# A four-layer graph network, 32 graphs on one core: scales read straight into rows, loads that yield to turned rows, a first chain by chunk, and a last layer 3 with features on partitions

## The chip, the cores and the metric

The kernel runs on one core of one Trainium2 chip. The core has five engines that work side by side, each through its own queue in order: TensorE (PE in the profile; PEld is its loading of weights) multiplies matrices, VectorE (DVE) and ScalarE (ACT) work on elements, GpSimd (POOL) does a few odd operations, and SyncE (SP) issues transfers (DMAs). An instruction that waits holds up everything behind it in its queue. Data live in SBUF and in eight PSUM banks, both with 128 partitions; a product takes its first operand (the weights, 128x128 here) and streams 128, 256 or 512 columns of the second past it.

The metric is the time of one execution on the device in microseconds (us), lower is better. All numbers are float32.

## The reference

There are 32 graphs ("batches") of N = 512 nodes with D = 128 features, and an adjacency matrix A (512x512) for each. Four layers follow one another; each normalizes x by rows, takes the positive part h, and adds its result to x. Cut to what matters:

```python
for layer in (L0, L1, L2, L3):
    h = relu(layernorm(x));  x = x + layer(h, A)

L0:  A1 = A + I;  r = rowsum(A1) ** -0.5
     leaky_relu((r A1 r) (h W) + b)
L1:  i, o, n = elu(h W_in + b), elu(h W_out + b), elu(h W_node + b)
     tanh([A i, n, A^T o] W_upd + b)
L2:  four sublayers on f (skip connections widen f to 1, 1, 2, 3 blocks of 128):
     f = tanh([rows_l2(A) (f ws + bs), f wn + bn, cols_l2(A)^T (f wd + bd)] wu + bu)
     # rows_l2 / cols_l2: each row / column divided by its Euclidean norm
L3:  m = tanh(A (h W_msg + b));  gi = m W_ih + b;  gh = h W_hh + b
     r, z = sigmoid(gi_r + gh_r), sigmoid(gi_z + gh_z)
     n = tanh(gi_n + r * gh_n);   out = (1 - z) * n + z * h
```

## The kernel before

**Data.** A batch's nodes are cut into four chunks of 128. `x`, `h` and the like are kept as rows (a node on each partition, four chunks side by side, 256 KB); `hT`, `f`, `agg` have features on partitions and 512 nodes along. The adjacency is read from memory twice, as `a` and as its transpose `aT` (1 MB each, by pieces of 256 KB for batch 0 and of 512 KB for the others), and `aT` a third time as `aT2` for layer 3, since layer 2 multiplies `a` and `aT` by its scales in place. An aggregation is four products of 512 columns into one bank (`ps_agg`). Layer 2's update weights are folded into the others at the start (`setup`, lines 334 to 417, from the tables `raw0`, `raw2`, `raw3`); three of its and layer 3's linear parts go by a scheme of seven products instead of eight (`seven`, lines 558 to 628).

**The order is planned.** `program(b)` does not issue anything: it records operations with `op(engine, us, ...)`, a guessed cost, what they read and write, and for a DMA its KB. `Plan.order` (lines 157 to 228) then simulates all engines and picks, on each engine, the ready operation with the smallest key:

```python
due = o.batch * PERIOD if o.batch < B - 1 else (B - 2) * PERIOD + ENDING
o.key = (due - o.tail + o.later if o.rank is None else o.rank - 1e6, i)
```

`tail` is the longest chain of costs behind an operation in its batch, `PERIOD` is 30, and `rank` puts the first loads ahead of all. Buffers come from slots (8 PSUM banks, 32 slots `s2` of 256 KB, 6 `s4` of 512 KB, 10 `s8` of 1 MB); an operation that needs a slot waits in the plan until one is free, and younger batches leave `kept` slots of each kind to older ones. So several batches are under way at once, and any change of costs, dependencies or slots can reorder every queue. `kept_warm` (line 235) puts idle products on PE where the plan has a gap of over 0.7 us. All DMAs are issued by SP, but for two small ones by ACT at the start.

**The steps that the change and the prediction touch**, by lines of the kernel before:

- `normed` (456 to 479): four row statistics on DVE (`moments`), variance to the power -0.5 on POOL into `sc` (line 466, 4 columns), the offset `nb` on DVE (474), and four normalizations `h` on ACT (478). For layer 0 the row sums of `a` come with it: `degree` (635) on ACT, four chunks of 512 columns, and the power then has 8 columns.
- `transposed` (510) gives `hT`. For batches 0, 1 and 31 by four transposing products on PE and a copy on ACT (516, 517). For all others by `turned` (483 to 501): DVE turns 32x32 blocks into `blk` (487), four DMAs of 64 KB write it to memory in another order (496), one DMA of 256 KB reads it back (500), and ACT puts the columns in order (519). The same path brings layer 2's result back to rows as `f4r`, where DVE adds it to x (784); the end batches use products instead (781).
- `own` (646): A + I needs the diagonal blocks of `aT` plus the identity: `diag`, on POOL, by chunk for batch 0.
- Layer 1: `ps_lin` is layer 0's last product, DVE applies scale and bias to it (`z`), then comes `normed`, `hT`, the products `ps_sd` of i and o, their exponents, and `rep` (691 to 695), on which the two aggregations wait. `u1` (706) is the update's sum on DVE.
- Layer 2's scales: ACT squares and sums `a` and `aT` by chunks (716 to 718), POOL takes the power -0.5 of 8 columns into `inv` (721), SP writes it to memory (`bounce`, 4 KB, line 726), and one DMA of 512 KB reads the 4 KB back to all partitions as `spaced` (730), where the 8 scales of a node lie side by side. ACT copies them apart into `rows` (735, 1024 columns), and DVE multiplies the eight chunks of `aT` and `a` by them (739). After that come four sublayers, each ended by a tanh on ACT (768).
- Layer 3: the message products and `msg`, the aggregation over `aT2`, `mT` (tanh, 801), the gate products (809 to 834) with nodes on partitions, tanh for r and z with halved arguments, and lines 842 to 859 for `u`, `n`, `w`, `q`, `xo` and the output DMA. In the last two batches this goes chunk by chunk, with the gates' biases added from broadcast rows (834), and with POOL doing two steps of `q`.

## Time and profile before

| what | us |
|---|---|
| median of nine runs | 2320.31 (2319.4 to 2323.42) |
| the profiled execution, its own time | 2321.19 |
| its span, first to last instruction | 2319.3 |
| PE busy, 9682 products | 2298.6 |
| DVE / ACT / POOL busy | 1530.4 / 946.9 / 262.0 |
| the 32 copies `rows` on ACT, each | 2.06 |
| `spaced`, issue to landing, median | 4.2 |
| `f4r`, issue to landing, median (shortest turned row read: `turned` 2.7) | 3.4 |

How to read it. The page gives each engine's busy time and its share of the span; a group's line reads: line, engine, operation, output<-inputs, shapes, count, busy time, mean in ns, idle time before it and what ended that. A timeline line reads: start in us, duration, engine, line, operation, and in brackets the idle time before it with what ended it; lines of SPq are issues of DMAs. A windows line gives the stretch, its length, and each engine's busy time with the number of instructions, then the granted TensorE clock (1.00 is full), the share of DMA time and GB/s. The granted clock is 0.999 over the whole span.

### The profile page before, as it was taken

What the parts mean: (1) busy time and instruction counts of PE and PEld (TensorE: products, weight loads), DVE (VectorE), ACT (ScalarE), POOL (GpSimd) and SP (SyncE); (2) the same over time, 40 slices, a digit from 0 to 9 for tenths busy, and PEclk for the clock granted to TensorE, in tenths of its full rate; (3) what the DMA queues carried; (4) which work ended last, traced back from release to release, by engine and by line L of the source; (5) the groups of instructions that cost most, each with busy time, mean ns of one, the idle gap of its engine ahead of it and who ended that gap; (6) DMA issues with size and microseconds to landing.
All of it is one profiled execution on the core that took longest, in us unless ns stands there. A gap on an engine that the chain in (4) does not pass through costs nothing.

```text
span 2319.3 us, 28279 instructions
## 1 busy us (share of the span) xinstructions
PE 2298.6 (99%) x9682; PEld 1445.2 (62%) x9682; DVE 1530.4 (66%) x4132; ACT 946.9 (41%) x2018; POOL 262.0 (11%) x218
## 2 busy tenths in 40 slices
PE   8999999999999999999999999999999999999998
PEld 7556666666666566666666665666666666656665
DVE  6656666666667676666666676766766666767655
ACT  8323444344443344343344433444433444334412
POOL 3001110101101011010111100110101111101101
PEclk9999999999999999999999999999999999999999
DMA  7102322223222233222332322322223322223200
GB/s 270 37 10 65 117 83 84 86 85 109 77 88 82 82 109 87 87 77 83 104 107 76 91 82 82 109 84 86 82 83 104 109 74 91 82 82 105 78 5 27
DMA packets 133054, 200.82 MB, mean 87 GB/s; under 512 B 18992, under 2 KB 79920, under 8 KB 132912
## 3 DMA queue, kind: packets, MB, share of 16 engines
q1 hardware_dynamic: 132624, 198.90, 28.3%
q8 instruction: 76, 1.25, 0.2%
q14 instruction: 66, 0.54, 0.1%
q10 hardware_dynamic: 288, 0.13, 0.0%
HBM read 160.05 MB, written 38.93 MB: 86 GB/s over the span
## 4 chain that ended last, share of the span: by engine, by line
PE 90%; DMA 4%; DVE 3%; ACT 2%; POOL 1%; SPq 1%; issue 0%; ACTq 0%; DVEq 0%
PE ps_agg L326 60%; PE ps_seven L597 11%; PE ps_sd L326 9%; PE ps_upd L326 4%; PE ps_gate L326 2%; DMA f4r<-turn_f4r 1%; PE ps_msg L326 1%; PE ps_node L326 1%; ACT h L478 1%; DMA turn_f4r<-blk 1%; PE ps_lin L326 1%; POOL sc L466 1%; SPq L496 1%; ACT f L768 1%; DVE bn L450 0%
## 5 line engine op out<-in xcount | busy, mean ns | idle before, releaser
L326 PE MATMUL ps_agg<-aT,sd 128*128 128x512 f32 x1024 | 510.2, 593 | 0.1
L326 PE MATMUL ps_agg<-a,sd 128*128 128x512 f32 x1024 | 482.4, 592 | 0.0
L466 POOL TENSOR_TENSOR sc<-v,neg_half 128x4 f32<-128x4 f32 (+1 forms) x128 | 157.7, 1232 | 1634.9 <-DVE v L453 1360.6
L326 PEld LDWEIGHTS ps_agg<-a,sd 128*128 128x128 f32 x1024 | 184.6, 190 | 182.9 <-issue 178.4
L326 PE MATMUL ps_agg<-f,w_sb 128*128 128x512 f32 x448 | 230.3, 596 | 5.4 <-ACT f L768 5.3
L326 PEld LDWEIGHTS ps_agg<-aT,sd 128*128 128x128 f32 x1024 | 177.9, 191 | 82.2 <-issue 66.0
L326 PE MATMUL ps_sd<-w_sb,f 128*128 128x256 f32 x768 | 217.4, 380 | 0.5 <-ACT f L768 0.4
L478 ACT ACTIVATE h<-xr,nb,sc 128x128 f32<-128x128 f32 x384 | 158.2, 482 | 136.6 <-DVE nb L474 136.3
L597 PEld LDWEIGHTS ps_seven<-t_sb,s 128*128 128x128 f32 x1128 | 161.5, 191 | 78.1 <-issue 69.3
L326 PEld LDWEIGHTS ps_sd<-w_sb,f 128*128 128x128 f32 x768 | 136.5, 191 | 95.3 <-issue 76.8
L597 PE MATMUL ps_seven<-t_sb,s 128*128 128x128 f32 x1128 | 168.1, 275 | 0.0
L735 ACT COPY rows<-spaced 128x1024 f32<-128x1024 f32 x32 | 66.1, 2064 | 169.9 <-DMA spaced<-bounce 169.9
L326 PE MATMUL ps_agg<-aT,rep 128*128 128x512 f32 x256 | 130.3, 593 | 2.0 <-DVE rep L693 2.0
L326 PE MATMUL ps_agg<-a,rep 128*128 128x512 f32 x256 | 130.4, 592 | 0.0
L768 ACT ACTIVATE f<-ps_agg,cf_sb 128x512 f32<-128x512 f32 x128 | 87.2, 682 | 98.7 <-PE ps_agg L326 98.7
L326 PE MATMUL ps_agg<-aT,msg 128*128 128x512 f32 x256 | 124.9, 592 | 0.0
L487 DVE STREAM_TRANSPOSE blk<-f 128x512 f32<-128x512 f32 x29 | 20.6, 711 | 139.8 <-ACT f L768 139.8
L326 PE MATMUL ps_agg<-aT,h 128*128 128x256 f32 (+2 forms) x384 | 99.1, 381 | 0.0
L597 PEld LDWEIGHTS ps_seven<-w_sb,f 128*128 128x128 f32 x512 | 75.9, 191 | 35.4 <-issue 27.7
L553 DVE TENSOR_TENSOR sd<-ps_sd,rf_sb 128x512 f32<-128x512 f32 x128 | 87.0, 680 | 15.6 <-PE ps_sd L326 15.6
L739 DVE TENSOR_TENSOR aT<-aT,rows 128x512 f32<-128x512 f32 x128 | 88.1, 688 | 13.6 <-PE ps_agg L326 13.6
L739 DVE TENSOR_TENSOR a<-a,rows 128x512 f32<-128x512 f32 x128 | 88.2, 690 | 13.1 <-PE ps_agg L326 13.0
(144 smaller groups left out, 3815.3 us busy)
## 6 DMA issues: line engine op xcount, KB each, us to landing
aT<-in_adjt SPq DMA_DIRECT2D x124, 512.0 KB, 5.2
a<-in_adj SPq DMA_DIRECT2D x62, 512.0 KB, 5.0
turn_turned<-blk SPq DMA_DIRECT2D x348, 64.0 KB, 1.8
turned<-turn_turned SPq DMA_DIRECT2D x87, 256.0 KB, 2.7
spaced<-bounce SPq DMA_DIRECT2D x32, 512.0 KB, 4.2
x<-in_x SPq DMA_DIRECT2D x32, 256.0 KB, 2.9
out<-xo SPq DMA_DIRECT2D x30, 256.0 KB, 2.0
turn_f4r<-blk SPq DMA_DIRECT2D x116, 64.0 KB, 1.8
```

The lines of the kernel that those rows point to most:

```text
L326: op("PE", t_mm(n), lambda: nc.tensor.matmul(out_of(ps.ap()), lhs(), rhs(), start=start, stop=stop), reads, [ps], later=later)
L466: op("POOL", t_pow(n), lambda: nc.gpsimd.tensor_tensor(inv.ap()[:, :n], v8.ap()[:, :n], neg_half[:, :n], op=ALU.pow), [v8, NH], [(inv, {0})])
L478: op("ACT", t_act(D, 2), lambda c=c: nc.scalar.activation(h.ap()[:, c, :], xin.ap()[:, c, :], AF.Relu, bias=nb.ap()[:, c:c + 1], scale=inv ...
L487: op("DVE", t_tt(N), lambda: nc.vector.transpose(blk.ap().rearrange("p b (c r) -> p c b r", c=NC), m.ap().rearrange("p c (b s) -> p c b s" ...
L496: nc.sync.dma_start(bounce.tile[:, k, :].rearrange("(b s) n -> s b n", b=NC), blk.ap()[k * P // NC:(k + 1) * P // NC])
L553: op("DVE", t_tt(N), lambda ps=ps, h=h: nc.vector.tensor_add(sd.ap()[:, 2 * h:2 * h + 2, :], ps.ap().rearrange("p (j v) -> p j v", j=2), s ...
L597: op("PE", t_mm(D), lambda j=j: nc.tensor.matmul(ps.ap()[:, k * H + j * D:k * H + (j + 1) * D], lhs()[:, j * P:(j + 1) * P], rhs(), start= ...
L735: op("ACT", t_act(2 * N), lambda: nc.scalar.copy(rows.ap().rearrange("p s (c n) -> p (s c) n", c=NC), spaced.ap().rearrange("p n k -> p k ...
L739: op("DVE", t_tt(N), lambda m=m, c=c, s=s: nc.vector.tensor_mul(m.ap()[:, c, :], m.ap()[:, c, :], rows.ap()[:, s, :]), [(m, {c}), rows], [ ...
L768: op("ACT", t_act(N, 1), lambda ps=ps, i=i, f_new=f_new: nc.scalar.activation(f_new.ap(), ps.ap(), AF.Tanh, bias=cf_sb[:, i:i + 1]), [ps, ...
```

## The change

The four parts of the title, and with them the plan's constants:

- **Scales.** `inv` is written into tiles of 32 columns, of which 24 are zeroed once by POOL. DVE turns them by blocks of 32x32, so that a scale's 32 nodes lie along a partition. 16 KB go to memory instead of 4, and the read to all partitions takes four pieces of 1 KB and lands in `rows` itself. The buffer `spaced` and the copy on ACT are gone; the eight multiplications read and write through a split view. There is one `s4` slot less and one `s2` more.
- **Loads yield.** A *way* is open in the plan from the turning of a row to its read back, and from the scales' power to the read of `rows`. While one is open, a load without a rank is not picked.
- **First loads.** `FIRST` lists the first 15 in order, with the loads of batches 1 and 2 among them; `aT` of batch 0 now goes ahead of `raw0`, `x` of batch 1 ahead of its `a`.
- **First chain by chunk.** In batch 0, `normed_by_chunk` sums each chunk of `a` on DVE, takes its power on POOL by one column, and makes offset and `h` for this chunk alone. `diag` is on DVE for batches 0 and 1.
- **Last batch.** `gates_turned` keeps layer 3's features on partitions: biases are added in ACT's function, nodes go in two halves, and products with plus or minus half the identity turn `q` and `nw` back to rows in PSUM, where DVE adds x. The output goes in two DMAs of 128 KB. Its bias columns come with `c_sb` (six more) and are copied and halved into `cg_sb` in `setup`.

The diff, cut (`...` where lines are left out; the older lines that are replaced are in the listing above):

```diff
-PERIOD = 30.0
+PERIOD = 28.0
+TURN = 32
+OWN = 2
+FIRST = ["x0", "a0", "aT0", "c", "raw0", "w1", "r1", "raw2", "raw3", "x1", "a1", "aT1", "x2", "a2", "aT2"]
...
+    def way(self, first, last):
+        first.opens += 1
+        last.closes += 1
...
                     item = heapq.heappop(queue)
+                    if item[1].yields and under_way:
+                        held.append(item)
+                        continue
...
+                under_way += o.opens - o.closes
...
-    ... {"bank": 8, "s2": 32, "s4": 6, "s8": 10}, {"bank": 2, "s2": 5, "s4": 0, "s8": 1})
+    ... {"bank": 8, "s2": 33, "s4": 5, "s8": 10}, {"bank": 1, "s2": 5, "s4": 0, "s8": 1})
...
     def t_pow(n):
-        return 0.9 + 0.1 * n
+        return 0.35 + 0.157 * n
...
+        op("DVE", 0.08, lambda: nc.vector.tensor_copy(cg_sb[:, 2:4], c_sb[:, C_L3 + 2:C_L3 + 4]), [CS], [CG])
+        op("DVE", 0.08, lambda: nc.vector.tensor_add(cg_sb[:, 0:2], c_sb[:, C_L3:C_L3 + 2], c_sb[:, C_L3 + 4:C_L3 + 6]), [CS], [CG])
+        op("DVE", 0.08, lambda: nc.vector.tensor_scalar_mul(cg_sb[:, 0:3], cg_sb[:, 0:3], 0.5), [CG], [CG])
...
+        def gates_turned(x3, h3T, msg, aT2, mT):
...
+            mm(ps, lambda t: t, lambda: wt(W_L3_HH + 2 * D), lambda: h3T.ap(), N, True, True, [h3T, W3])
+            ... hn.ap(), ps.ap(), AF.Identity, bias=cg_sb[:, 2:3], scale=0.5)
+            for k in range(2):      # halves of 256 nodes: aggregation, then mT = tanh
...
+            for k in range(2):
+                gate(ps_r, 0, W_L3_HH, h3T, True, False)
+                gate(ps_z, 0, W_L3_HH + D, h3T, True, False)
+                gate(ps_r, 0, W_L3_IH, mT, False, True, part)
+                gate(ps_n, 0, W_L3_IH + 2 * D, mT, True, True, part)
+                gate(ps_z, 0, W_L3_IH + D, mT, False, True, part)
+                act(rp, ..., AF.Tanh, 0, [ps_r], scale=0.5)
+                u = (rp + 1) * hn;  u = u + ps_n                      # two DVE steps
+                act(zp, ..., AF.Tanh, 1, [ps_z], scale=0.5)
+                act(n, lambda s=s: u.ap()[:, s], AF.Tanh, 3, [(u, part)])
+                q = (zp + 1) * h3T;  nw = (zp - 1) * n                # two DVE steps
+                for src, turn, start in ((q, 0, True), (nw, 1, False)):
+                    for j in range(2):
+                        mm(ps_o[j], ..., src[block 2k+j], id_half[turn], D, start, not start, ...)
+                for j in range(2):
+                    xo[2k+j] = x3[2k+j] + ps_o[j]                     # DVE
+                op("SP", 0.4, ... dma_start(out[b][:, 2 * k:2 * k + 2, :], xo ...), kb=H / 2)
...
         def load(dst, src, kb, rank):
+            name = f"{rank}{b}"
+            rank, kb = first(name), kb * (2 if name == "a0" else 1)
...
-                   [], [(dst, set(range(NC)[s]))], kb=kb / pieces, rank=None if b else rank)
+                   [], [(dst, set(range(NC)[s]))], kb=kb / pieces, rank=rank, yields=rank is None)
...
+        def normed_by_chunk(xin, out_tag):
...
+            for c in range(NC):
+                op("DVE", t_tt(N), ... tensor_reduce(stat.ap()[:, c:c + 1], a.ap()[:, c, :], AX.X, ALU.add), ...)
+                v8[NC+c] = stat[c] + 1                                # DVE
+                op("POOL", t_pow(1), ... inv[NC+c] = v8[NC+c] ** neg_half)
+                inv[2NC+c] = inv[c] * inv[NC+c];  nb[c] = -mean[c] * inv[2NC+c]   # two DVE steps
+                h[c] = Relu(xin[c] * inv[2NC+c] + nb[c])              # ACT
...
+            plan.way(m.uses[0][0], back)
...
-        hr, inv0 = normed(xt, "h", degree)
+        hr, inv0 = normed_by_chunk(xt, "h") if b < 1 else normed(xt, "h", degree)
...
+        own_engine, own_name = (nc.vector, "DVE") if b < OWN else (nc.gpsimd, "POOL")
...
-        bounce, spaced, rows = buf("bounce", (P, 2 * NC)), buf("s4", (P, P, 2 * NC), "spaced"), buf("s4", (P, 2, N), "rows")
+        bounce, rows = buf("bounce", (P, TURN)), buf("s4", (P, NC, 2, NC, TURN), "rows")
+        op("DVE", 0.1, lambda: nc.vector.transpose(turned_inv.ap(), inv.ap()), [inv], [turned_inv])
...
-            nc.sync.dma_start(spaced.ap().rearrange("p n k -> p (n k)"),
-                              bass.AP(tensor=d.tensor, offset=d.offset, ap=[[0, P], [1, 2 * N]]))
+            nc.sync.dma_start(rows.ap().rearrange("p q s c r -> p q (s c r)"),
+                              bass.AP(tensor=d.tensor, offset=d.offset, ap=[[0, P], [TURN * TURN, NC], [1, 2 * P]]))
...
-        op("ACT", t_act(2 * N), lambda: nc.scalar.copy(
-            rows.ap().rearrange("p s (c n) -> p (s c) n", c=NC), spaced.ap().rearrange("p n k -> p k n")), [spaced], [rows])
...
+        plan.way(root, op("SP", 0.4, spread, [bounce], [rows], kb=640))
...
+        if b == B - 1:
+            gates_turned(x3, h3T, msg, aT2, mT)
+            return
```

(Lines such as `u = (rp + 1) * hn` stand for an operation written out in full in the code.)

## The prediction, made before the changed kernel had run

> **What bounds the kernel now.** I read the page first: is one engine full, and where is it not?
>
> ```profile
> span 2319.3 us, 28279 instructions
> PE 2298.6 (99%) x9682; PEld 1445.2 (62%) x9682; DVE 1530.4 (66%) x4132; ACT 946.9 (41%) x2018; POOL 262.0 (11%) x218
> ```
>
> PE is busy 99% of the span, so only three things can shorten the kernel: less PE work, PE idle time, and the tail after PE's last product. The change leaves PE's work per batch as it is, so the second and third are what can be had. The windows view (PE busy first, then PEld, DVE, ACT, POOL, clock, DMA) says where PE idles.
>
> ```profile
> 500.00:1000.00 500.00, 496.39 (x2076) 310.37 (x2075) 336.31 (x904) 205.72 (x435) 54.97 (x42) 1.00 0.30 89
> 1000.00:1500.00 500.00, 499.52 (x2090) 312.77 (x2089) 339.83 (x910) 206.48 (x435) 54.50 (x42) 1.00 0.30 91
> 1500.00:2000.00 500.00, 499.96 (x2087) 312.28 (x2086) 340.89 (x914) 207.17 (x436) 54.94 (x42) 1.00 0.30 90
> ```
>
> The steady part loses almost nothing late and 3.6 us early. All windows from 60 to 2200 us together lose 6.4 us, and eight rows of idle products at 263.9 hide 0.9 more: 7.3 us. What ends these waits, by the waits view (us, times, longest) and one of the places in the timeline:
>
> ```profile
> PE ps_agg L326 <- ACT f L768: 5.3, 7, 1.5
> PE ps_agg L326 <- DVE rep L693: 2.0, 1, 2.0
> ```
>
> ```profile
> 341.58 0.39 SPq L730 DMA_DIRECT2D spaced<-bounce  x1
> 342.89 0.34 SPq L500 DMA_DIRECT2D f4r<-turn_f4r  x1
> 347.68 0.69 DVE L784 TENSOR_TENSOR xr<-xr,f4r 128x512 f32<-128x512 f32 x1 [1.55 <-DMA f4r<-turn_f4r]
> 351.91 1.65 ACT L478 ACTIVATE h<-xr,nb,sc 128x128 f32<-128x128 f32 x4 [1.46 <-DVE nb L474]
> 353.47 0.67 ACT L768 ACTIVATE f<-ps_agg,cf_sb 128x512 f32<-128x512 f32 x1
> 354.19 1.13 PE L326 MATMUL ps_agg<-f,w_sb 128*128 128x512 f32 x2 [0.98 <-ACT f L768]
> ```
>
> 512 KB of `spaced` go out 1.3 us ahead of the turned rows `f4r`, which land 4.8 us after issue; DVE waits 1.55, four normalizations reach ACT late and stand ahead of the tanh that PE waits for.
>
> The start: 33.3 us of PE work (the products before layer 2's first, by number, at 0.857 us for 512 columns, 0.43 for 256, 0.22 for 128) end at 55.2 us: 22 us lost.
>
> ```profile
> 9.87 1.65 POOL L466 TENSOR_TENSOR sc<-v,neg_half 128x8 f32<-128x8 f32 x1 [8.53 <-DVE v L640]
> 13.26 0.46 PE L326 MATMUL ps_agg<-diag,h 128*128 128x128 f32 x2 [0.93 <-ACT h L478]
> 30.47 2.06 ACT L735 COPY rows<-spaced 128x1024 f32<-128x1024 f32 x1 [0.46 <-DMA spaced<-bounce]
> 33.93 1.69 DVE L693 TENSOR_TENSOR rep<-rep,sd 128x512 f32<-128x512 f32 x1
> 35.68 1.12 PE L326 MATMUL ps_agg<-aT,rep 128*128 128x512 f32 x2 [1.99 <-DVE rep L693]
> ```
>
> The end: PE's last products start at 2311.5, and what follows takes 7.7 us.
>
> ```profile
> 2307.00 0.58 ACT L801 ACTIVATE mT<-ps_agg 128x512 f32<-128x512 f32 x1
> 2310.78 1.04 PE L326 MATMUL ps_gate<-w_sb,mT 128*128 128x128 f32 x6
> 2315.81 0.48 DVE L857 TENSOR_TENSOR xo<-q,n 128x128 f32<-128x128 f32 x2
> ```
>
> **The change part by part. Start.** The degrees move from ACT (0.63 us and a 0.19 us read each) to a DVE reduction a chunk. No row has it: between 0.43 (tensor-scalar, 512 columns) and 0.69 (tensor-tensor); I take 0.65. The one-column root lies between nothing and the 1.01 of four columns; the slope to the eight-column 1.65 gives 0.5. Last chunk of `a`: landed at 8.7, root at 10.4. But `aT` rules: its last chunk lands at 13.2 now and, with 768 KB of `raw0` behind it instead of ahead (1.9 us at the queue's 410 GB/s), at 11.3. A new copy of `c_sb` into `cg_sb` stands in DVE's queue ahead of the last two chunks and waits for `c_sb`, which lands at 11.4 now. Then two `diag` (0.28), the small ones and h (0.49): aggregation over at 14.0 instead of 17.0, so 3.0 us. From there to the products on `rep` (18.7 us now) I take off 0.7 (x of batch 1 lands before a), 1.1 (nb took 1.22 beside POOL's diag, 0.15 elsewhere; diag is on DVE here), 0.4 (copies ahead of hT), 1.3 (the 2.06 us rows copy ahead of the exponent), 1.0 (L693 was 1.69 beside POOL, 0.68 elsewhere), and add 1.2 for batch 1's diag and batch 2's statistics, which now stand ahead of `sd` on DVE and wait for their loads: products on rep at 29.4, 6.3 us earlier. Back comes 1.1: the eight multiplications by `rows` now stand ahead of `u` on DVE, and `rows` lands near 34.5, its bounce queued behind batch 2's loads: 29.8, plus 4.7 like the first `spaced` (4.88). Start: **-5.2**, between -3 (DMA rules) and -7.5 (nothing comes back).
>
> By the Trainium skill (TensorE: Matmul & The Clock Gate, What's actually happening) an idle window of about 3.4 us halves PE's clock, which speaks against 43 idle products instead of 60. Here the 1.99 us gap was followed by full-speed products, and every slice's granted clock is 9. Were a gap to pass the limit, an estimate from that page is +1.7 us.
>
> **Scales of layer 2.** Gone in each batch: the 2.06 us ACT copy; `spaced` (512 KB) moves from ahead of `f4r` to behind it. Added: a 32-column DVE transpose (between 0.13, the smallest op, and 0.71 for 512 columns; 0.15), 16 KB out instead of 4 (1.4 us to landing now; 64 KB take 1.8), and rows in pieces of 1 KB (4.2 now). Multiplications with a split view: L784 reads and writes such a view at 0.68, as L739 does its plain one at 0.69, so nothing. The rows are issued some 10 us before their readers.
>
> The Trainium skill (DMA: Bandwidth & Descriptors, Anatomy of one DMA; Specifications) gives 2.0 us plus bytes over 436 GB/s, so an estimate of 3.2 us for rows against the row's 4.2, and a penalty under 512 bytes a piece, which the bounce's 128 bytes fall under. Either leaves the readers covered, and the sum as it is.
>
> With f4r alone in the queue (2.85 us like `turned`, not 3.4 to 4.8), and layer 2's tanh ahead of f4r's normalizations on ACT, the seven ACT waits should go, and the idle at 264. The early batches (1 to 3) keep waits of their own. I take **-6.0** of 7.3, between -7.3 and -2.
>
> **The new order's own risk.** It differs in each of some 26 like batches, so a small wait counts 26 times. The tightest turned row I find is layer 1's:
>
> ```profile
> 844.61 1.11 POOL L466 TENSOR_TENSOR sc<-v,neg_half 128x4 f32<-128x4 f32 x1 [10.24 <-DVE v L453]
> 852.56 0.34 SPq L500 DMA_DIRECT2D turned<-turn_turned  x1
> 855.45 0.62 ACT L519 COPY hT<-turned 128x512 f32<-128x512 f32 x1 [3.56 <-DMA turned<-turn_turned]
> 856.88 1.03 PE L326 MATMUL ps_sd<-w_sb,hT 128*128 128x256 f32 x4
> ```
>
> From layer 0's last product (838.9) hT took 17.2 us; PE reached it at 18.0 and did not wait. In the new order PE has 14 products of 512, 3 of 256 and 17 of 128 columns between (17.0 us) instead of 13, 4 and 23 (17.9). The chain: the stream transpose of f now stands ahead of z on DVE (+0.35), sd for s (+0.2), 0.85 of other work leaves, POOL's 1.65 us root for the scales stands ahead of sc (sc at 5.95, not 5.75), and nb no longer waits behind f4r's xr (-0.8): hT at 16.7, usable at 16.85. Slack 0.15 instead of 0.7. If rows slows the four DMAs behind it as spaced slowed f4r (0.55), PE waits 0.4; if not, 0. The rows issue is 2 us ahead, so nearer to none: 0.06 a batch, **+1.5**, between 0 and +10.
>
> **Last batch.** Its products: 10 of 256, one of 512 and 8 of 128 columns for 8 and 8, +1.7 us, of which 0.9 lies in the new tail. Before the tail: 0.9 of idle products goes, 0.9 of products comes. Tail after the last gate product: 0.2, tanh 0.45, tanh 0.42, nw 0.42, products 0.6, additions 0.5, signals 0.4, then 2.6 from the last issue to the end as now: 5.6 against 7.45 now. **-1.9**, between +0.5 and -3.5.
>
> Loads that yield to turned rows: their bytes stay; slots free them 20 us and more before use in the steady part, so nothing.
>
> Sum: -5.2 - 6.0 + 1.5 - 1.9 = -11.6. The profiled execution took 2321.2 (span 2319.3 and 1.9 around it), its nine runs' median 2320.3: 2309.6 on the one, 2308.7 on the median. I say 2308.5.
>
> **Rivals.** First, *slower*: hT's wait. It alone decides from 0.5 us a batch, where 26 waits eat the 13.1 us of the other terms; at 0.65 the time is 2324. For it: a slack of 0.15 in a 17 us chain, and 512 KB ahead of four small DMAs. Against it: those rows are sent 2 us ahead, and f4r cost only 0.55 at 1.3 us. Second, *the queue rules the start*: the DMA's share is 0.94 to 1.04 from 10 to 40 us, so a shorter chain could only wait for loads: -2 instead of -5.2, 2312. Third, *the change does not do it in the middle*: f4r stays late behind out and adjacency loads, -1 instead of -6: 2314. Fourth, *all of it, no new wait*: -7.5 - 7.3 - 3.5 gives 2302.
>
> **How the numbers follow.** No change can be told within 0.2%, 4.6 us. Forecast with its spread (2303 to 2313) 0.47; the queue or the middle (2310 to 2315.5) 0.21; all of it (2298 to 2303) 0.10; a wait at hT of 0.25 to 0.5 us that leaves 2315.7 to 2322, 0.12; more than that, 0.10. Faster 0.78, same 0.10, slower 0.12 (some of the same lies near its upper bound). For 8 in 10 the range goes from 2300 to 2319.
>
> **What would show it.** Right: PE's products on rep near 29, the first layer-2 product near 50, no waits for ACT f in the middle, 1500 to 2000 as full as before, out's last issue some 3 us after the last product. Wrong: a wait of PE ps_sd for ACT hT 26 times; DVE waiting for DMA rows ahead of u well past 36; DVE stuck on c_sb past 12. The prediction falls if the period of a middle batch (70.7 us now) grows by 0.4 or more.

## The result, and the profile after

The changed kernel takes 2328.9 us (median; 2323.53 to 2334.32), where the kernel before, run beside it, took 2321.09 (2318.64 to 2323.87). The ratio is 1.0032, 95% interval 1.0024 to 1.0039: slower by 0.3%, where 2308.5 was forecast. The profiled execution took 2327.39, with a span of 2325.6 and a granted clock of 0.999 over it. The differences between traces below are differences of spans, 2319.3 and 2325.6: +6.3.

The page's first lines, of the kernel after:

```profile
span 2325.6 us, 28292 instructions
...
PE 2303.3 (99%) x9662; PEld 1443.2 (62%) x9662; DVE 1530.5 (66%) x4179; ACT 872.2 (38%) x1970; POOL 260.5 (11%) x210
```

PE is 99% busy as before, and ACT's busy time fell by 74.7 us, most of it the copies (66.1). PE's own busy time grew by 4.7 with 20 instructions fewer (each product of the program is two instructions here), which says nothing yet: the ends of products are modelled, and part of a wait can count as busy. So I compared the starts of PE's products: the time at which PE has done a given amount of work (number of products of each kind by their undisturbed times), less that work, is what is lost up to there.

| stretch, by PE's work | lost, before | lost, after | change | forecast |
|---|---|---|---|---|
| start, first 60 us of work | 22.85 | 19.51 | -3.3 | -5.2 |
| middle, 60 to 2150 us | 22.8 | 35.7 | +12.9 | -4.5 |
| end (lost -0.5, more products +1.7, tail after the last product's start -4.4) | | | -3.2 | -1.9 |
| sum | | | +6.4 | -11.6 |

Start and end gave what was promised, 6.5 us against 7.1. The middle went the wrong way by 17.4 us. Its three windows of after, with the columns of the prediction's:

```profile
500.00:1000.00 500.00, 497.84 (x2076) 310.09 (x2075) 336.47 (x913) 190.47 (x429) 56.23 (x42) 1.00 0.30 91
1000.00:1500.00 500.00, 496.60 (x2071) 308.96 (x2070) 334.15 (x909) 189.16 (x427) 55.97 (x42) 1.00 0.29 88
1500.00:2000.00 500.00, 495.71 (x2070) 308.87 (x2069) 333.76 (x908) 188.62 (x426) 56.24 (x42) 1.00 0.29 88
```

Before, the third window was full (499.96); here it is the emptiest. What PE waits for, by the waits view of after (us, times, longest):

```profile
PE ps_sd L350 <- ACT hT L638: 8.1, 12, 2.0
PE ps_agg L350 <- DVE msg L917: 3.5, 5, 1.0
PE ps_agg L350 <- DVE rep L813: 2.9, 2, 2.5
...
PE ps_agg L350 <- ACT f L891: 0.2, 1, 0.2
```

The wait for layer 2's `f` (5.3, seven times) is down to one of 0.2. In its place stand `hT` of layer 1, `msg` of layer 3, and `rep`. The starts show more than the waits view, since products behind the late one run slow too: from 70 to 2260 us, hT costs 14.1, msg 5.4, and rep with the products behind it 4.5; against that 9.4 of waits for f and of idle products went, and some 0.8 elsewhere. That closes the balance: 24.0 - 9.4 - 0.8 = 13.8, which is the growth in that stretch.

**hT.** One of the twelve places, in the timeline of after:

```profile
1770.98 0.37 SPq L853 DMA_DIRECT2D rows<-bounce  x1
1772.87 1.82 SPq L614 DMA_DIRECT2D turn_turned<-blk  x4
1778.94 0.34 SPq L618 DMA_DIRECT2D turned<-turn_turned  x1
1781.84 0.62 ACT L638 COPY hT<-turned 128x512 f32<-128x512 f32 x1 [5.66 <-DMA turned<-turn_turned]
1782.51 1.78 PE L350 MATMUL ps_sd<-w_sb,hT 128*128 128x256 f32 x7 [2.02 <-ACT hT L638]
```

The 512 KB of `rows` go out 1.9 us ahead of the four writes of 64 KB that turn layer 1's rows. SP can issue the read back only when the writes have landed; that is 6.1 us after the first write here, and 3.3 in the kernel before (median). The order is the same in all batches 4 to 30, and the times in nearly all: rows 7.7 us after the last product of layer 0, the writes at 9.65, and PE arrives at 17.1. The DMA issues show it in the medians (KB each, median us from issue to landing), first of before, then of after:

```profile
turn_turned<-blk SPq DMA_DIRECT2D x348, 64.0 KB, 1.8
...
spaced<-bounce SPq DMA_DIRECT2D x32, 512.0 KB, 4.2
...
x<-in_x SPq DMA_DIRECT2D x32, 256.0 KB, 2.9
```

```profile
turn_turned<-blk SPq DMA_DIRECT2D x348, 64.0 KB, 2.3
...
rows<-bounce SPq DMA_DIRECT2D x32, 512.0 KB, 5.3
...
x<-in_x SPq DMA_DIRECT2D x32, 256.0 KB, 6.0
...
f4r<-turn_f4r SPq DMA_DIRECT2D x29, 256.0 KB, 2.6
```

The same 512 KB take 1.1 us longer as `rows` than as `spaced`, and x takes twice as long.

**msg.** On DVE, the statistics of x of the batch after next stand some 10 us ahead of msg. Where x is late, DVE stands still, and in all five places of a wait for msg PE's product on msg starts 10.68 us after x has landed. One of DVE's waits for x:

```profile
1360.63 0.29 DVE L542 BATCH_NORM_STATS2 bn<-x 128x6 f32<-128x128 f32 x1 [3.20 <-DMA x<-in_x]
```

**The last batch.** Here `rows` go out 1.3 us ahead of the read of f4r, just as spaced did in the kernel before (timeline, then windows of after):

```profile
2192.67 0.38 SPq L853 DMA_DIRECT2D rows<-bounce  x1
2193.95 0.34 SPq L618 DMA_DIRECT2D f4r<-turn_f4r  x1
2199.85 0.69 DVE L907 TENSOR_TENSOR xr<-xr,f4r 128x512 f32<-128x512 f32 x1 [4.07 <-DMA f4r<-turn_f4r]
2203.71 1.83 PE L350 MATMUL ps_agg<-aT,rep 128*128 128x512 f32 x2 [2.46 <-DVE rep L813]
```

```profile
2202.00:2204.00 2.00, 0.29 (x1) 0.30 (x2) 2.00 (x6) 1.65 (x4) 0.00 (x0) 0.99 0.00 0
2204.00:2206.00 2.00, 2.00 (x3) 0.68 (x2) 2.00 (x5) 0.26 (x1) 0.00 (x0) 0.50 0.03 8
```

f4r lands 5.9 us after its issue instead of the median 2.6, `rep` stands behind it, PE waits 2.46, and then the granted clock is 0.50: the wait is paid a second time by products at half speed.

**Start and end**, in the timeline of after:

```profile
11.35 0.17 DVE L387 COPY cg_sb<-c_sb 128x2 f32<-128x2 f32 x1 [0.98 <-DMA c_sb<-in_bcol]
13.91 0.38 PE L350 MATMUL ps_agg<-diag,h 128*128 128x128 f32 x2
29.96 1.13 PE L350 MATMUL ps_agg<-aT,rep 128*128 128x512 f32 x2 [0.42 <-DVE rep L813]
42.21 0.16 DVE L589 TENSOR_TENSOR sc<-sc 128x4 f32<-128x4 f32 x1 [0.33 <-POOL sc L584]
42.89 0.68 DVE L826 TENSOR_TENSOR u<-ps_upd,r_sb 128x512 f32<-128x512 f32 x1
51.91 1.13 PE L350 MATMUL ps_sd<-w_sb,f 128*128 128x256 f32 x4
...
2319.32 1.03 PE L350 MATMUL ps_gate<-mT,w_sb 128*128 128x256 f32 x4
2321.37 0.71 PE L350 MATMUL ps_gate<-id_half,q 128*128 128x128 f32 x4
```

The products on rep come 5.7 us earlier than before; the first layer-2 products only 3.3, since `u` stands on DVE behind `sc` of batch 1.

### The profile page after: what moved, and what is told of

The parts are those of the page before. It is cut to its first block, busy times and chain, and to the rows that moved or that the text cites. A ratio compares the mean times of both kernels' runs of the same rounds, so it can differ in the third digit from the quotient of the medians.

```text
span 2325.6 us, 28292 instructions
## 1 busy us (share of the span) xinstructions
PE 2303.3 (99%) x9662; PEld 1443.2 (62%) x9662; DVE 1530.5 (66%) x4179; ACT 872.2 (38%) x1970; POOL 260.5 (11%) x210
## 4 chain that ended last, share of the span: by engine, by line
PE 80%; DMA 8%; DVE 6%; POOL 2%; SPq 2%; ACT 1%; issue 1%; ACTq 0%; POOLq 0%; DVEq 0%
PE ps_agg L350 53%; PE ps_seven L716 10%; PE ps_sd L350 8%; PE ps_upd L350 3%; PE ps_gate L350 3%; DMA turn_turned<-blk 3%; DMA x<-in_x 2%; DMA turned<-turn_turned 1%; SPq L614 1%; POOL sc L584 1%; DVE bn L542 1%; PE ps_msg L350 1%; PE ps_lin L350 1%; PE ps_node L350 1%; DVE sd L672 1%
## 5 line engine op out<-in xcount | busy, mean ns | idle before, releaser
L350 PE MATMUL ps_agg<-aT,sd 128*128 128x512 f32 x1024 | 503.9, 593 | 0.4 <-DVE sd L694 0.3
L350 PE MATMUL ps_agg<-a,sd 128*128 128x512 f32 x1024 | 501.9, 593 | 0.0
L350 PEld LDWEIGHTS ps_agg<-a,sd 128*128 128x128 f32 x1024 | 175.9, 191 | 114.8 <-issue 112.9
L716 PEld LDWEIGHTS ps_seven<-t_sb,s 128*128 128x128 f32 x1128 | 167.3, 191 | 92.6 <-issue 84.4
L965 ACT ACTIVATE g<-g 128x512 f32<-128x512 f32 (+1 forms) x64 | 36.1, 608 | 399.4 <-DVE g L694 398.9
L716 PE MATMUL ps_seven<-t_sb,s 128*128 128x128 f32 x1128 | 178.6, 275 | 0.0
L742 DVE TENSOR_TENSOR ev<-ps_seven,ev 128x512 f32<-128x512 f32 x94 | 65.0, 691 | 132.0 <-PE ps_seven L716 131.7
L350 PE MATMUL ps_agg<-aT,msg 128*128 128x512 f32 (+1 forms) x264 | 131.4, 583 | 3.5 <-DVE msg L917 3.5
L841 POOL TENSOR_TENSOR inv_sb<-stat,neg_half 128x8 f32<-128x8 f32 x32 | 53.0, 1657 | 677.8 <-DVE stat L840 653.3
L837 ACT ACTIVATE sq<-aT 128x512 f32<-128x512 f32 x128 | 80.1, 626 | 49.2 <-DMA aT<-in_adjt 48.2
```

Of the source, the lines that this page charges most:

```text
L350: op("PE", t_mm(n), lambda: nc.tensor.matmul(out_of(ps.ap()), lhs(), rhs(), start=start, stop=stop), reads, [ps], later=later)
L716: op("PE", t_mm(D), lambda j=j: nc.tensor.matmul(ps.ap()[:, k * H + j * D:k * H + (j + 1) * D], lhs()[:, j * P:(j + 1) * P], rhs(), start= ...
L742: op("DVE", t_tt(N), lambda: nc.vector.tensor_add(ev.ap(), bank_b.ap()[:, None, :H].to_broadcast([P, 2, H]), ev.ap()), [bank_b, ev], [ev])
L837: op("ACT", 0.73, lambda c=c, s=s, m=m: nc.scalar.activation(sq.ap(), m.ap()[:, c, :], AF.Square, accum_out=stat.ap()[:, s * NC + c:s * NC ...
L841: root = op("POOL", t_pow(2 * NC), lambda: nc.gpsimd.tensor_tensor(inv.ap()[:, :2 * NC], stat.ap(), neg_half, op=ALU.pow), [stat, NH], [inv])
L965: op("ACT", t_act(cols), lambda s=s: nc.scalar.activation(g.ap()[:, s, :2 * D], g.ap()[:, s, :2 * D], AF.Tanh, scale=0.5), [(g, fields(par ...
```

## The experiments

Each ran beside the kernel before on its chip; there the kernel before has medians from 2318.8 to 2321.3 us, so the ratios are what is compared. "Late" is how much later products start than they could, by the starts of products as above.

### Is the place of rows in the queue the cause?

The first kernel sends `rows` of batches 4 to 30 behind the next read back, the second behind the one after that; the order on all other engines stays.

```diff
-        plan.kept_warm(plan.order(), idle_products, 1.3)
+        plan.kept_warm(behind(plan.order(), lambda o: o.tag == "rows" and 3 < o.batch < B - 1, "back"), idle_products, 1.3)
```

> Change to the changed kernel: in SP's queue alone, the read of rows of batches 4 to 30 goes behind the read back of the turned row that follows it (layer 1's hT), so ahead of the four writes of the second turned row. Every other queue is as in the changed kernel (median 2328.9 us). Theory A, rows ahead of the four writes holds up layer 1's turned row: hT's waits, 14 us of PE's time in the changed kernel's trace, are gone, the four writes land 3.1 us after their first issue instead of 3.7 to 6.0. But now the second turned row's writes stand 0.4 us behind rows, the loads behind it come 1.5 us later, x lands later, DVE waits longer for it, and msg comes late in most batches instead of 5 of 27: 20 to 35 us of new waits, in all 2335 to 2350 us. Theory B, the changed order's own chain on DVE, POOL and ACT makes hT late: hT's waits stay at some 14 us, and the time is 2328 to 2350 us with PE still waiting for hT.

> As the run before, but rows goes behind the second turned row's read back too, directly ahead of the loads. Theory A: no writes of turned rows stand behind rows any more, hT's waits (14 us) are gone; the loads are issued some 0.6 us earlier than in the changed kernel but have 512 KB, 1.3 us, ahead of them, and PE comes 0.5 us earlier to msg, so x is late by about 0.5 us in many batches: msg's waits go from 5 us to some 5 to 14. In all 2316 to 2329 us. Theory B: hT's waits stay, 2329 us or more.

Measured: 2354.84, ratio 1.0158 (1.0144 to 1.0171), and 2367.72, 1.0208 (1.0194 to 1.0222). The waits view of the first, then of the second:

```profile
PE ps_agg L364 <- DVE msg L934: 21.3, 24, 1.0
...
PE ps_sd L364 <- ACT hT L653: 0.9, 2, 0.6
```

```profile
PE ps_agg L366 <- DVE msg L936: 24.5, 25, 1.0
PE ps_upd L366 <- ACT agg_in L835: 11.6, 16, 1.8
...
PE ps_sd L366 <- ACT hT L655: 1.4, 2, 0.7
```

hT is late by 1.4 and 1.9 us in all instead of 14.1: rows ahead of the writes is what made it late. But the wait moves to whatever comes behind rows: the loads of the second kernel land 8.0 (`a`) and 8.6 us (`x`) after issue instead of 5.1 and 6.0, and the msg waits, five in after, become 24 and 25. The sizes were missed, in the second kernel by some 40 us. Whoever stands behind `rows` loses 2 to 3 us (in the first kernel the writes right behind it, 5.4 us to landing instead of 3.1), far more than I had charged; so the question became what makes them so slow.

### Is it the form of the read?

The first kernel reads one piece of 4 KB for each partition instead of four of 1 KB. It takes the first 4 KB of the bounce, which are not the scales of all nodes, so its results are not the reference's; the work and its order are the same.

```diff
...
-    ap=[[0, P], [TURN * TURN, NC], [1, 2 * P]]
+    ap=[[0, P], [1, 2 * N]]
```

> One size: rows is read as one piece of 4 KB for each partition (128 pieces) instead of four of 1 KB (512 pieces), 512 KB as before, at the same place in the queue. It reads the first 4 KB of the bounce, so layer 2's scales are wrong; the work and its order are the same. If the number of pieces makes rows slow and so the writes behind it late: rows lands 4.2 us after its issue (like spaced in the kernel before) instead of 5.3, the writes behind it 0.5 to 1 us earlier, and hT's waits fall from 14 us to under 5: 2318 to 2322 us. If only the bytes count: rows 5 us or more, the same 2326 to 2332 us.

Measured: 2307.04, 0.9947 (0.9933 to 0.996), better than had been expected. `rows` take 3.7 us, the four writes 3.1 from first issue to landing, hT is late by 2.6 in all, msg by 2.8. The windows view of one us of such a read (the last two columns are the DMA engines' busy share and GB/s), of after and then of this kernel:

```profile
1057.00:1058.00 1.00, 1.00 (x9) 0.82 (x8) 0.55 (x3) 0.63 (x1) 0.48 (x1) 1.00 0.59 172
```

```profile
1050.00:1051.00 1.00, 1.00 (x4) 0.44 (x3) 1.00 (x6) 0.34 (x1) 0.00 (x0) 1.00 0.72 279
```

The next kernel has the right scales with that read: four small writes put them close together, and the last batch's rows go behind f4r.

```diff
-    nc.sync.dma_start(bounce.tile, turned_inv.ap())
+    for q in range(NC):
+        nc.sync.dma_start(bounce.tile[q], turned_inv.ap()[q * TURN:q * TURN + 2 * NC])
```

> A version that computes everything and reads rows in one piece of 4 KB for each partition: the scales are written by four DMAs of 1 KB (8 partitions each) so that they lie together, and the last batch's rows goes behind f4r. All other queues are as in the changed kernel. The three more issues on SP put rows some 1.1 us later, so 0.8 us ahead of the first turned row's writes instead of 1.9. If the pieces are the cause: rows lands under 4.2 us after issue, the writes behind it in some 3.3 us, hT's waits under 3 us, 2306 to 2311 us. If it is the distance of a 512 KB read from the writes that counts, they are held up more than before, 4 us and over, and hT waits in every batch: 2320 to 2335 us.

Measured: 2311.0, 0.9959 (0.9946 to 0.9971). The gain holds with the right scales. hT is late by 1.7 in all; msg still by 5.8, so the speed of rows is not all that makes msg late.

Is it the number of pieces, or their size? Two pieces of 2 KB (again not the scales of all nodes), and then four DMAs of 128 KB with one piece each:

```diff
...
-    ap=[[0, P], [TURN * TURN, NC], [1, 2 * P]]
+    ap=[[0, P], [2 * TURN * TURN, 2], [1, 4 * P]]
```

```diff
+    for q in range(NC):
+        nc.sync.dma_start(rows.ap()[:, q]...,
+                          bass.AP(..., offset=d.offset + q * TURN * TURN, ap=[[0, P], [1, 2 * P]]))
```

> As the run with one piece of 4 KB at the same place in the changed kernel's queue, but with two pieces of 2 KB for each partition (256 pieces, 512 KB); the scales of layer 2 are wrong again. Pieces of 1 KB: landed 5.2 us after issue, the writes behind in 3.9, hT's waits 5 to 12 us, 2319 to 2329 us. Pieces of 4 KB: 3.7, 3.1, 2 us, 2307 us. If the time goes with the number of pieces, 4.2 us to landing and hT's waits of 2 to 4 us: 2308 to 2313 us. If a limit lies between 1 and 2 KB: as with 4 KB, 3.7 us, 2305 to 2309 us.

> The changed kernel with rows read by four DMAs of 128 KB, one piece of 1 KB for each partition in each, instead of one DMA with four pieces. It computes everything. The pieces and their places in memory stay; SP issues three DMAs more, so the writes behind them start up to 0.5 us later. Theory P: each DMA has one piece for each partition and is spread over all engines: the last part lands 4.5 us or less after the first issue, the writes behind in 3.3 us, hT's waits 2 to 4 us, 2308 to 2313 us. Theory S, or 1 KB pieces as such: packets of rows still some 8 at a time, 5 us or more, 2320 to 2330 us.

Measured: 2324.81, 1.0015 (1.0006 to 1.0024), and 2327.45, 1.0037 (1.0024 to 1.005). Half the pieces at double size still take 5.1 us, and four DMAs leave hT late by 11.9 and msg by 8.9. Neither number nor size nor the one DMA explains it. What is left is where the pieces lie. The next reads the same four pieces of 1 KB, but 1040 bytes apart instead of 4096; the one after that 2560 apart. Both thus read other numbers than the scales:

```diff
-    ap=[[0, P], [TURN * TURN, NC], [1, 2 * P]]
+    ap=[[0, P], [2 * P + 4, NC], [1, 2 * P]]      # the other kernel: [5 * P, NC]
```

> The changed kernel with one number changed: the four 1 KB pieces of rows are read 1040 bytes apart in memory instead of 4096 (the scales of layer 2 are wrong; work, order and number of pieces are the same). In the changed kernel some 8 packets of rows are in flight at a time and 512 KB take 3 us, with one piece of 4 KB 13 packets and 1.3 us. Theory S, pieces 4096 (or, with 2 KB, 8192) bytes apart meet in the same part of the memory: now 3.7 to 4.2 us to landing, 2306 to 2312 us. Theory P, several pieces for each partition in one DMA are spread badly over the engines: 5 us or more to landing, 2319 to 2329 us.

> The changed kernel with the four 1 KB pieces read 2560 bytes apart (scales wrong), so over 8.5 KB, at 0, 2560, 1024 and 3584 within stretches of 4096 bytes. Place within 4096 counts: 4.2 us to landing, 2306 to 2312 us. The length of the stretch counts: between the 4.1 us of 4 KB and the 5.2 of 13 KB, 2311 to 2329 us.

Measured: 2310.05, 0.9966 (0.9955 to 0.9978), and 2316.57, 0.9988 (0.9979 to 0.9996). The first differs from after in one number of one access, in no queue's order and no instruction's shape. The DMA issues of the first, then of the second:

```profile
rows<-bounce SPq DMA_DIRECT2D x32, 512.0 KB, 4.1
```

```profile
rows<-bounce SPq DMA_DIRECT2D x32, 512.0 KB, 4.8
```

That can be had with the right scales by leaving room between the blocks in memory. 64 bytes of room (pieces 4160 apart); the same with a later place for x's statistics (below) and the last batch's rows behind f4r; and 1024 bytes (5120 apart):

```diff
-    bounce.tile = dram.tile([P, TURN], ...)
+    bounce.tile = dram.tile([NC, TURN * TURN + APART], ...)      # APART = 16, or 256 numbers
...
-    ap=[[0, P], [TURN * TURN, NC], [1, 2 * P]]
+    ap=[[0, P], [TURN * TURN + APART, NC], [1, 2 * P]]
```

> The changed kernel, complete, with one constant added: in memory 64 bytes are left free behind each group of 32 rows of the bounce, so that the four 1 KB pieces of rows lie 4160 bytes apart instead of 4096. Nothing else moves. If pieces a multiple of 4096 apart meet in the same part of the memory: rows lands some 4.1 us after issue, the writes behind it in 3.1 us, hT's waits 1 to 3 us, 2306 to 2312 us. If it is only that at 1040 bytes the pieces lie within one stretch of 4 KB and so were already open: 5 us to landing, 2320 to 2330 us.

> The same with x's statistics behind mT on DVE and the last batch's rows behind f4r. With padding 3 issues fewer on SP than in the version with one piece of 4 KB that took 2306.7: rows again 1.9 us ahead of the writes. If the padding does it: 2303 to 2307 us. If not: 2315 to 2322 us, as with x's statistics alone.

> As the padded kernel, complete, but with 1024 bytes left free instead of 64, so that the four pieces of rows lie 5120 bytes apart. With 4160 they were as slow as with 4096, and 4160 leaves them in nearly the same place within a stretch of 4096 bytes. If it counts where a piece lies within 4096 bytes (0, 1024, 2048, 3072 here, as with one piece of 4 KB or with pieces 1040 apart): rows lands in 4.2 us, 2308 to 2313 us. If it counts over how long a stretch the pieces are spread (16 KB, as in the changed kernel): 5 us, 2324 to 2340 us.

Measured: 2337.72, 1.0079 (1.0065 to 1.0093); 2327.7, 1.0035 (1.0022 to 1.0048); and 2311.51, 0.9961 (0.9947 to 0.9975). The first two are slower than both expectations. So 64 bytes do next to nothing for the speed (5.0 us). In the first, the bounce also takes longer to issue (0.52 us instead of 0.34), rows come only 1.27 us ahead of the writes, and hT is late by 21.7; 1024 bytes cure it (4.0 us, hT late by 1.9 in all).

| pieces for a partition | bytes apart | issue to landing | hT late | ratio |
|---|---|---|---|---|
| 4 of 1 KB (after) | 4096 | 5.3 | 14.1 | 1.0032 |
| 2 of 2 KB | 8192 | 5.1 | 10.4 | 1.0015 |
| 4 of 1 KB, padded | 4160 | 5.0 | 21.7 | 1.0079 |
| 4 of 1 KB | 2560 | 4.8 | 5.8 | 0.9988 |
| 4 of 1 KB | 1040 | 4.1 | 1.5 | 0.9966 |
| 4 of 1 KB, padded | 5120 | 4.0 | 1.9 | 0.9961 |
| 1 of 4 KB | | 3.7 | 2.6 | 0.9947 |

Of the two rules on trial in the last expectations, the length of memory that the pieces span fails: 5120 apart they span 16 KB and are quick. The place of each piece within 4096 bytes fits all rows but one: pieces 2560 apart were expected quick and took 4.8. There the first and the last piece share 512 of the 4096 bytes (the last one starts at 3584), which may be why; no run here shows it.

By the Trainium skill (DMA: Bandwidth & Descriptors, Latency and other measured facts) copies whose rows lie 2 to 8 MiB apart run at 164 down to 103 GB/s; with 4 MiB, 4 KiB of padding restore the full rate of 214 where 192 bytes don't; why is called an inference there. The runs agree in kind, at distances down to 4096 bytes, with 64 bytes of padding useless and 1024 enough. Which part of the memory is in the way is not shown here either.

### Do the loads that yield matter, and whence the msg waits?

Without the hold, all else as in after:

```diff
-                    if item[1].yields and under_way:
-                        held.append(item)
-                        continue
```

> The changed kernel with the rule that loads yield taken out of the plan, so that the order changes again: layer 3's aT goes ahead of f4r's writes, x between f4r's writes and its read, a behind the third turned row. The 1 KB pieces of rows still stand ahead of layer 1's turned row. Theory A (rows is the cause, yielding is not): hT's waits stay at 7 to 14 us, the waits for msg (x late) go, and PE waits for the tanh of layer 2 again because f4r has 1 MB ahead of it, 5 to 10 us: 2325 to 2338 us. Rival, the loads that yield are what made the turned rows and x late: hT's waits and msg's go, under 2318 us.

Measured: 2353.95, 1.0149 (1.0133 to 1.0165), the waits view:

```profile
PE ps_sd L347 <- ACT hT L635: 25.0, 27, 2.2
PE ps_agg L347 <- DVE sd L691: 8.5, 16, 0.6
```

That is slower than either expectation, and the waits for f did not come back. The yield is not the harm as a whole: without it layer 2's turned rows queue behind 1 MB of adjacency (5.1 us for their writes), all that follows comes later, `rows` go out 1.5 us ahead of layer 1's writes and these some 10 to 12 us after layer 0's last product instead of 9.65, and hT is late in every like batch. But x lands in 4.2 us instead of 6.0, and the msg waits are gone. The yield lets loads pile up and go in one burst, in which x takes 5.5 to 6.8 us (medians) in all kernels that have it and whose page gives a landing, but for the one with rows ahead of the loads (8.6). So I left the burst alone and moved who waits for x: for batches 5 to 30 its statistics go behind the tanh `mT` in the plan's order, and thus behind msg on DVE. First in after, then in the kernel with pieces of 4 KB:

```diff
+            if 4 < b < B - 1:
+                for o in plan.ops[first_op:first_op + 2 * NC + 1]: o.tag = "xstat"
...
-        plan.kept_warm(plan.order(), idle_products, 1.3)
+        plan.kept_warm(behind(plan.order(), lambda o: o.tag == "xstat", "mT"), idle_products, 1.3)
```

> The changed kernel, rows in pieces of 1 KB as there, with only x's statistics moved behind mT on DVE. Theory (rows makes the turned rows late, these make the loads late since SP issues in order, and DVE stands on x ahead of msg): msg's waits, 5 to 10 us in the two traces of the changed kernel, go, hT's waits of 7 to 14 us stay: 2315 to 2322 us where the changed kernel has 2324 to 2329. If a's load stands behind it, msg's waits stay: 2322 to 2329 us.

> The complete version with rows in one piece of 4 KB (2311.0 us, of which its trace has 5.8 us of PE waiting for msg) with one more edit: the statistics of x of the batch after the next (four bn_stats, four bn_aggr, one addition on DVE, which stood some 10 us ahead of msg and waited for x to land) go behind the tanh mT, just ahead of the DVE operation that waits 2 us for it. SP, PE, ACT and POOL keep their queues. Theory: msg is late because DVE stands on x; its waits go, 2305 to 2308 us. Rival, msg is late for the load of a, through ACT's sums: msg's waits stay at 3 us or more, 2309 to 2312 us.

Measured: 2320.32, 1.0000 (0.9991 to 1.0009), and 2306.68, 0.9938 (0.9926 to 0.9951). In both the msg waits are gone (0.1 and 0.0 late). hT stays late by 13.2 in the first. So the two waits go separately: x, landing late and standing on DVE ahead of msg, makes msg late; rows ahead of the writes makes hT late. rows have a hand in x too, as the 8.6 us show.

### The parts alone

The last batch's rows behind the read of f4r (the first edit with `o.batch == B - 1`), the kernel after once more, and the kernel before with nothing but `gates_turned` and its columns of `c_sb`:

```diff
+        plan.kept_warm(behind(plan.order(), lambda o: o.tag == "rows" and o.batch == B - 1, "back"), idle_products, 1.3)
```

```diff
+        if b == B - 1:
+            gates_turned(x3, h3T, msg, aT2, mT)
+            return
         psa = plan.bank("agg")
```

> Only the last batch's read of rows is moved in SP's queue, from ahead of the read back of f4r to behind it. In the profiled execution f4r took 5.9 us there instead of 2.6, DVE stood 4.1 us on it with the layer 1 work of the last batch behind it, PE waited 2.46 us for rep, and the next 2 to 3 us of products ran at a granted clock of 0.50. Theory A (rows holds up f4r): f4r lands 3 us after issue, the wait and the slow clock are gone, 4 to 5 us less where it happens: 2324 to 2326 us. Rival, the two loads of 512 KB behind f4r hold it up and rows does not: f4r still over 5 us, no change, 2328 to 2330 us.

> The changed kernel itself, beside the next three. The last batch's rows moved behind f4r gave 2318.7 us where the changed kernel had 2328.9, 10 us, while its trace explains only 5 (a wait of 2.5 us for rep and some 2 us of products at half clock) and shows hT's waits 5 us shorter for no reason in the edit. If one edit in the last batch is worth 10 us, this repeat is at 2326 to 2332 us. If the waits for hT, which hang on how fast the 1 KB pieces of rows go, differ from chip to chip by some us, it is at 2320 to 2325 us, with hT's waits between 7 and 12 us.

> The kernel before with one part of the change alone: the last batch's layer 3 with features on partitions. All queues are those of the kernel before up to the last batch. The prediction's term for it was 1.9 us less, between 0.5 more and 3.5 less. The changed kernel's trace has its end 3.3 us after PE's last product instead of 7.7, with 1.7 us more of products, so 2.7 us less, and another 1.5 us less lost by PE in the last 20 us. Theory A: the end is worth 2.7 to 4.2 us, 2316 to 2318.5 us beside 2320.5 for the kernel before. Rival, the end's gain belongs to the rest of the new order: 2319 us or more.

Measured: 2318.7, 0.9999 (0.999 to 1.0008); 2324.06, 1.002 (1.001 to 1.003); and 2316.23, 0.9983 (0.9974 to 0.9992). In the first the wait for rep and the half clock are gone, but hT was late by 9.2 and not 14.1 in that profile, so how much of the 10 us against after is the edit's, and how much the spread between chips and profiles, is not settled. After again had msg late by 10.2 and hT by 6.9, the reverse of the first profile: how the two split varies from one profile to another, and the 2.04 us gap ahead of rep was not followed by a lower clock. The new last layer alone is worth 3.8 us, twice my 1.9.

### Everything together

1024 bytes of room, x's statistics later, and the last rows behind f4r:

```diff
+APART = 256                      # as in the kernel with pieces 5120 apart
...
+        plan.kept_warm(behind(behind(plan.order(), lambda o: o.tag == "xstat", "mT"),
+                              lambda o: o.tag == "rows" and o.batch == B - 1, "back"), idle_products, 1.3)
```

> The complete kernel with 1024 bytes left free (pieces of rows 5120 bytes apart, 2311.5 us, of which 6.4 us are PE's waits for msg), with x's statistics behind mT on DVE and the last batch's rows behind f4r. If DVE standing on x is what makes msg late here too: 2304 to 2307 us, as with one piece of 4 KB and the same two edits (2306.7). If a's load stands behind it: 2309 to 2312 us.

Measured: 2305.32 (2303.86 to 2306.33), 0.9937 (0.9924 to 0.9951): 14.3 us faster than before on that chip. No other version was faster; the one with pieces of 4 KB and x later is its equal (0.9938). Its page, its windows and its waits for hT:

```profile
PE 2293.7 (100%) x9662; PEld 1445.0 (63%) x9662; DVE 1541.9 (67%) x4179; ACT 872.5 (38%) x1970; POOL 257.6 (11%) x210
```

```profile
500.00:1000.00 500.00, 499.65 (x2094) 313.06 (x2093) 341.41 (x917) 191.53 (x429) 57.77 (x43) 1.00 0.29 89
1000.00:1500.00 500.00, 500.00 (x2109) 314.47 (x2108) 341.42 (x923) 193.21 (x433) 55.09 (x42) 1.00 0.29 89
1500.00:2000.00 500.00, 498.44 (x2085) 311.65 (x2084) 341.38 (x919) 191.41 (x431) 56.57 (x43) 1.00 0.28 89
```

```profile
PE ps_sd L368 <- ACT hT L657: 1.6, 2, 1.0
```

From 60 to 2150 us of work it loses 14.1 us, where before lost 22.8 and after 35.7. That is the 8.7 us gain in the middle that the change as written did not give; I had forecast 4.5.

## Why the prediction was wrong

The time fell outside the range, on the side of the first rival and past its price. By its steps:

- **Start: right in the chain, short in the end.** `c_sb` was waited for until 11.35 (11.4 forecast), the aggregation was over at 14.3 (14.0), and the products on rep started at 29.96 (29.4). What comes back before layer 2 was charged at 1.1 and measured 2.4, for a reason I had not named: the forecast had the multiplications by `rows` ahead of `u`, and in the trace it stands behind `sc` of batch 1 as well, for which POOL's power ended at 42.2. With 4 KB pieces rows landed at 35.1 instead of 37.4, POOL still ended at 42.2, and `u` still started at 42.90; why POOL was no earlier there is open. So -3.3 instead of -5.2.
- **The waits for f: right.** f4r's way from first write to landing shrank from 6.75 to 6.10 us (median) and its read from 3.4 to 2.6; the seven waits are one of 0.2. By the starts 9.4 us went, idle products included, so the term of -6.0 came in and more; it was paid back elsewhere.
- **The slack at hT: right for PE, too small for the chain.** PE reached it at 17.11 (17.0 forecast). Where rows were quick (3.7 and 4.1 us, in the same order) hT was ready at 16.1 (medians) and not at 16.7, so the slack was some 0.9 us and not 0.15. It was lost all the same: in after hT was ready at 17.3.
- **The failed step: "rows in pieces of 1 KB (4.2 now)".** I took spaced's 4.2 us for rows. They take 5.3, because their pieces lie 4096 bytes apart (spaced was read in one stretch of 4 KB, the form that takes 3.7 us in rows' place). On that rests "If rows slows the four DMAs behind it as spaced slowed f4r (0.55), PE waits 0.4; if not, 0. The rows issue is 2 us ahead, so nearer to none: 0.06 a batch": a read of over 5 us, issued 1.9 us ahead, is still under way while the writes go, and these landed 3.7 to 6.0 us after their first issue (median 4.1) instead of 3.1. That is 1 us in the median where I had 0.55 at most and said "nearer to none". hT cost 14.1 us over 27 batches, 0.52 a batch, against 0.06, and past the term's bound of +10: the first rival's mechanism at the first rival's price (it was to decide from 0.5). The other kernels bear it out: with rows of 3.7 to 4.1 us in the same place of the queue, hT costs 1.5 to 3.3. The 3.2 us that I had estimated from the Trainium skill missed by more. The page (DMA: Bandwidth & Descriptors, Anatomy of one DMA) gives that fit for transfers that GpSimd issues, and rows are issued by SP.
- **"Loads that yield: ... nothing": wrong in both directions.** The bytes do stay, but the burst makes x late, and x stands on DVE ahead of msg: 5.4 us that no term or rival named. I had asked who waits for the loads' slots, and not who waits in which queue for their landing. Without the yield the products from 70 to 2260 us start late by 62.6 us in all, with it by 37.0.
- **The last batch's middle: not in the sum.** I had rows move from ahead of f4r to behind it "in each batch"; in batch 31 they stayed 1.3 us ahead of it. It gave a wait of 2.46 us, and about 2 us more of products at half speed.
- **End: right in sign, short in size.** The tail after the last gate product took 5.6, as worked out; ahead of it more was gained, so -3.2 in the profiled pair and -3.8 alone, where -1.9 was forecast. That start and end together came within 0.6 us of their forecast is luck in part: one was 1.9 short, the other 1.3 better.

With hT at its measured 14.1 in place of 1.5 the forecast's sum is +1.0, some 2321 us: this one term turns a gain into none and leaves the range. The rest of the way to 2328.9 is above all msg (5.4) and rep (4.5), which stood in no term. rows' time was taken as one number from another transfer of the same bytes, and where the pieces lie was not asked.

## What to carry to other kernels

Before a large transfer is moved within a queue, price it by the layout that it will have, and list what is issued within its landing time behind it: it is these small transfers, and whoever waits in order for them, that pay. Where many partitions read the same few pieces of memory, keep the pieces next to each other, or test another distance: one number in an access was worth some 0.7% of the whole kernel here. And when loads are held back to let something pass, look for the engine that stands in its queue in front of their landing.

## What the runs showed of the hardware

**A broadcast read depends on how far apart its pieces lie.** 512 KB to 128 partitions, each from the same 4 KB: 5.0 to 5.3 us from issue to landing with pieces 4096, 4160 or 8192 bytes apart, 4.8 at 2560, and 3.7 to 4.1 at 1040, 5120 or in one piece. By the packets' own times, the 512 packets of 1 KB took 3.8 us from the first to the last in after (138 GB/s, medians of batches 4 to 30), 2.7 us 1040 apart (194 GB/s) and 2.5 us 5120 apart (211 GB/s).

**The clock dropped after shorter gaps than I had thought.** By the idle times that the profiles of these kernels give ahead of PE's products, none of the fifteen gaps of 1.30 to 1.76 us was followed by a lower granted clock, but of the 23 gaps of 1.83 to 2.63 us twelve were, to 0.51 to 0.75 over the next 2.5 us. The shortest of the twelve is 1.84 us, and after a gap of 2.55 us the clock stayed at 1.00. The Trainium skill (TensorE: Matmul & The Clock Gate, What's actually happening) has an idle window of about 3.4 us that runs freely; the traces here show the drop with less idle time than that, and not at a fixed length. What decides between two gaps of equal length, no run here shows.
